# A graph layer on one core: the node loops' stores on SyncE's queue, merged weight loads, and a new layout of the node loops' tiles

## The chip, the cores and the metric

The kernel runs on one NeuronCore of a Trainium2 chip. A core has a tensor engine (TensorE, PE in the profile) for matmuls into PSUM (eight banks of 2 KiB per partition), VectorE (DVE), ScalarE (ACT) and GpSimd (POOL) for elementwise work, and SyncE (SP), which only issues DMAs. Each engine runs its own list of instructions in order, and they wait for each other by semaphores. The metric is the device time of one execution in microseconds; lower is better. All data are float32.

## The reference

The input is x, 32 graphs of 512 nodes with 256 features, and adj, a 0/1 matrix of 512 by 512 for each graph. With h = relu(layernorm(x)), the layer computes:

```python
h1 = relu(bn(conv1d(h, conv1_w)))                     # width 1
x_conv = relu(bn(conv1d(h1, conv2_w, pad=8)) + h)     # width 17
s = h @ w_se.T + b_se                                 # 3 numbers a node
A = exp(-|s_n - s_m|^2) * adj                         # 512 x 512 for each graph
x_nmp = A @ relu(h @ w_msg.T + b_msg)
gi = concat(x_conv, x_nmp) @ w_ih.T + b_ih
gh = h @ w_hh.T + b_hh
r, z = sigmoid(gi_r + gh_r), sigmoid(gi_z + gh_z)
n = tanh(gi_n + r * gh_n)
out = x + (1 - z) * n + z * h
```

## The kernel before

The 32 graphs ("blocks") are worked on in two groups of 16 (NG = 2, GB = 16). The wide convolution is done by frequency: windows of 64 tokens are transformed to 80 rows, two rows make a unit (40 units), each unit is multiplied by its own 256 x 256 complex weight matrix, and the result is transformed back in the last part.

The program runs through five stretches. `first_part(0)` normalises and transforms blocks 0 to 15 and also brings the convolution weights to frequency: it stores them to DRAM (`wd`) from tiles `wst`. `nodes(0)` does the message passing of these blocks and, between it, the products of 36 units. `first_part(1)` does blocks 16 to 31, the four left units of group 0, and combines the gate weights in tiles `w4` and `w7`, from where they go to DRAM (`ws`). `nodes(1)` does the second group with all its 40 units. Then a loop over 16 pairs of blocks computes the gates. The change concerns the two node loops.

The order of the work is written out by hand (`manual_schedule`): each engine's instructions, and the DMAs of each queue, stand in the order in which the Python code names them. What the framework adds is semaphores and the places of tiles. Tiles with one tag of a pool share its buffers, and tags get their places in the order in which they are first asked for. A pool opened after another was closed takes its memory, and the first writer of a new tile waits for what still used the old tile in the same bytes. So the pool `nodes`, where adj, msg, st, sl, sr, A and at live, starts where `w2p` and then `wst` lay in the phase before the first loop, and where `x`, `h1`, `w4` and `w7` lay before the second.

In the node loop (lines 1037 to 1133), `todo` lists the 16 blocks. For each block: `load_adj` brings adj (four DMAs of 256 KB), `load_h` brings the transposed h, `by_chunks` copies it in another order to hq (ScalarE), `message` (L442 to L446) makes msg and the three features st, `features` puts them into fl and fr (VectorE), `factors` transposes these (psl, psr) and copies them to sl and sr (ScalarE), `exponents` makes the exponentials A, `turn` transposes adj to at and `masked` multiplies A by it (VectorE), `block_sums` forms sums of blocks of A and msg (GpSimd, L517), `aggregate7` multiplies them with seven block products instead of eight (L542 to L562) into nmp, and `save_nmp` stores nmp. The last blocks of the second loop use `aggregate` without sums. The work on the next blocks (`more[0]`, `more[1]`, ...) is laid between the matmuls of the present one.

Units are laid between: `multiply(u)` runs `product` (matmuls L390, the result y finished by ScalarE and VectorE), prepares unit u + 2 on GpSimd (wsum L357 and both L370), and loads the weights of a later unit into one of three buffers wt. The store of y is put into a list `stores`, and `flush()` issues what is in it. All stores of y (L400 to L404, issued in L1053) and of nmp (L565) are issued by ScalarE; all loads by SyncE:

```python
store = partial(nc.scalar.dma_start, YD[g][:, 2 * u : 2 * u + 2, :], y)   # L400
nc.scalar.dma_start(ND[b], NMP.pop(b))                                    # L565
nc.sync.dma_start(t[:, k], WD[2 * u + k, : D * D]...)                     # L353, k = 0, 1
```

Buffers: adj 2, msg 3, st 2, wt 3, y 3, hq 2, hT 2, nmp 1.

Of the kernel before, what the change touches and what calls it, by code (L numbers as in the profile page):

```python
# [15 lines left out]
P = 128  # L16
# [49 lines left out]
def gnn_layer(  # L66
# [282 lines left out]

    def load_unit(g, u, pool=wts):  # L350
        t = WT[g, u] = pool.tile([P, 2, DC, D], FP, tag="wt", name=f"wt_{g}_{u}")
        for k in range(2):
            nc.sync.dma_start(t[:, k], WD[2 * u + k, : D * D].rearrange("(p i o) -> p i o", i=DC, o=D))  # L353

    def sum_unit(pw, g, u):
        t = WSUM[g, u] = pw.tile([P, DC, D], FP, tag="wsum", name=f"wsum_{g}_{u}", bufs=2)
# [15 lines left out]
    def product(pw, g, u, xf, later=None):  # L372
        if u > 0 and (g, u) not in BOTH or (g, u) not in WT:
            prepare(pw, g, u, xf)
        wt = WT.pop((g, u))
        re, im = factors_of(xf, u)
        wr, wi = wt[:, 0], wt[:, 1]

        y = pw.tile([P, 2, D], FP, tag="y", name=f"y_{g}_{u}", bufs=3)
        p = bank(f"py_{g}_{u}")  # L380
        k1, k2 = p[:, :D], p[:, D:]
        if u == 0:
            terms = [(k1, re, wr), (k2, im, wi)]
        else:
            both, wsum = BOTH.pop((g, u)), WSUM.pop((g, u))
            k3 = bank(f"py2_{g}_{u}")[:, :D]
            terms = [(k1, re, wr), (k2, im, wi), (k3, both, wsum)]
        for dst, v, w in terms:
            for ic in range(DC):
                nc.tensor.matmul(dst, v[:, ic, :], w[:, ic, :], start=(ic == 0), stop=(ic == DC - 1))  # L390
        y_re, y_im = (by_half(y[:, k, :]) for k in range(2))
        if u == 0:
            nc.scalar.copy(y_re, halves(k1))
            nc.scalar.copy(y_im, halves(k2))
        else:
            nc.scalar.copy(y_re, halves(k1))
            nc.scalar.mul(y_im, halves(k1), -2.0)
            nc.vector.tensor_sub(y_re, y_re, halves(k2))
            nc.vector.tensor_add(y_im, y_im, halves(k3))
        store = partial(nc.scalar.dma_start, YD[g][:, 2 * u : 2 * u + 2, :], y)  # L400
        if later is None:
            store()
        else:
            later.append(store)  # L404

    def load_adj(b):
        ADJ[b] = pools["nodes"].tile([P, N // 32, P], FP, tag="adj", name=f"adj_{b}", bufs=2)

        rows = adj[b].rearrange("(j r) (g m) -> g r j m", r=32, g=4)
        for g in range(4):  # L410
            nc.sync.dma_start(ADJ[b][32 * g : 32 * (g + 1)], rows[g])

    def load_h(b):
        HT[b] = work.tile([P, DC, N], FP, tag="hT", name=f"hT2_{b}")
        nc.sync.dma_start(HT[b], HD[b])
# [13 lines left out]

    def message(b, halves=range(2)):  # L430
        if 0 in halves:
            MSG[b] = pools["nodes"].tile([P, NC, D], FP, tag="msg", name=f"msg_{b}", bufs=3)
            ST[b] = pools["nodes"].tile([P, 2, NC, NS], FP, tag="st", name=f"st_{b}", bufs=2)
        hq = HQ[b]
        h = NC // 2
        for c0 in (h * k for k in halves):
            m = MSG[b][:, c0 : c0 + h, :]
            for j in range(h):
                c = c0 + j
                p = bank(f"pm_{b}_{c}")  # L440
                for ic in range(DC):
                    nc.tensor.matmul(p[:, : D + NS], hq[:, ic, c * P : (c + 1) * P], wmsg[:, ic, :],  # L442
                                     start=(ic == 0), stop=(ic == DC - 1))
                nc.vector.tensor_add(ST[b][:, 0, c, :], p[:, D : D + NS], bmsg[:, D:])
                nc.vector.tensor_add(m[:, j, :], p[:, :D], bmsg[:, :D])
            nc.scalar.activation(m, m, AF.Relu)  # L446
        if 1 in halves:
            del HQ[b]
# [11 lines left out]
    def factors(b):  # L460

        p = bank(f"psl_{b}")
        nc.tensor.transpose(p[:, :P], fl.rearrange("p c k -> p (c k)"), ident)
        t = SL[b] = pools["nodes"].tile([P, P], FP, tag="sl", name=f"sl_{b}", bufs=2)
        nc.scalar.copy(t, p[:, :P])
        p = bank(f"psr_{b}")
        for c in range(NC):
            nc.tensor.transpose(p[:, c * P : (c + 1) * P], fr[:, c].rearrange("p g k -> p (g k)"), ident)  # L468
        t = SR[b] = pools["nodes"].tile([P, N], FP, tag="sr", name=f"sr_{b}", bufs=2)
        nc.scalar.copy(by_chunk(t), chunks(p))  # L470
# [91 lines left out]
        nc.vector.tensor_add(c21, p1, y)  # L562

    def save_nmp(b):
        nc.scalar.dma_start(ND[b], NMP.pop(b))  # L565

# [304 lines left out]
    def store(p, j, queues, t=slice(0, N)):  # L873
        js = slice(t.start // 32, t.stop // 32)
        for g in range(4):
            queues[g % len(queues)].dma_start(quarter(out[2 * p + j], g)[:, js], XP[p][j][32 * g : 32 * (g + 1), js])
# [126 lines left out]
    with tc.tile_pool(name="freq", bufs=1) as fpool:  # L1003
# [33 lines left out]
        def nodes(g, xf, units, last, following=()):  # L1037


            b1 = (g + 1) * GB  # L1040
            pw = pools["pw"]
            todo = [b1 - 1, b1 - 2] + list(range(g * GB, b1 - 2))
            loads = [u for u in (*units, *following) if (g, u) not in WT]
            stores = []

            def load_units(n):
                for _ in range(n):
                    if loads:
                        load_unit(g, loads.pop(0))

            def flush():
                while stores:
                    stores.pop(0)()  # L1053

            def multiply(u):
                product(pw, g, u, xf, stores)
                if u + 2 in units:
                    prepare(pw, g, u + 2, xf)
                load_units(1)

            load_adj(todo[0])
            load_units(3 - sum((g, u) in WT for u in units))
            load_adj(todo[1])
            load_h(todo[3])
            message(todo[0])
            features(todo[0])
            for step in message_sums(todo[0]):
                step()
            message(todo[1], [0])
            factors(todo[0])  # L1070
            message(todo[1], [1])
            features(todo[1])
            exponents(todo[0])
            by_chunks(todo[2])
            turn(todo[0], [0, 1])
            masked(todo[0], [0, 1])
            turn(todo[0], [2, 3])
            masked(todo[0], [2, 3])
            prepare(pw, g, units[1], xf)
            for step in affinity_sums(todo[0]):  # L1080
                step()
            for i, b in enumerate(todo):
                mine = spread(units, i, last) if i < last else []
                more = todo[i + 1 : i + 5]
                seven = i <= last

                def bring():
                    if len(more) > 1:
                        message(more[1])
                        flush()  # L1090
                        features(more[1])

                if g + 1 < NG and i == GB // 2:
                    load_x(b1)
                if g + 1 < NG and i == 3 * GB // 4:
                    statistics(b1)
                if len(more) > 1:
                    load_adj(more[1])
                if len(more) > 3:
                    load_h(more[3])  # L1100
                if more:
                    factors(more[0])
                flush()
                if i == 0:
                    bring()
                for u in mine[:1]:
                    multiply(u)
                if i > 0:
                    bring()
                if not seven:  # L1110
                    aggregate(b, [0])
                if more:
                    turn(more[0], [0, 1])
                    exponents(more[0])
                    masked(more[0], [0, 1])
                for u in mine[1:2]:
                    multiply(u)
                if more:
                    turn(more[0], [2, 3])
                    masked(more[0], [2, 3])  # L1120
                if seven:
                    aggregate7(b)
                else:
                    aggregate(b, [1])
                flush()
                if len(more) > 2:
                    by_chunks(more[2])
                save_nmp(b)
                if more and i + 1 <= last:
                    block_sums(more[0])  # L1130
                for u in mine[2:]:
                    multiply(u)
            flush()
# [105 lines left out]
```

## Time and profile before

The median of three runs is 1842.39 us (1841.37 to 1847.45); the profiled execution has a span of 1842.2 us.

| engine | busy us | share of the span | instructions |
|---|---|---|---|
| PE (matmul) | 1804.6 | 98% | 6974 |
| DVE | 1240.2 | 67% | 2370 |
| POOL | 776.0 | 42% | 731 |
| ACT | 622.0 | 34% | 1252 |

| stretch of the program | from about, us | to about, us |
|---|---|---|
| first_part(0) | 0 | 157 |
| nodes(0) | 157 | 455 |
| first_part(1) | 455 | 572 |
| nodes(1) | 572 | 877 |
| gates, pair by pair | 877 | 1842 |

The DMAs that the change touches, from the table of DMA issues (queue, number, size, median time from issue to landing):

| DMA | queue | count | KB each | us to landing |
|---|---|---|---|---|
| wt from wd | SyncE | 160 | 256 | 4.9 |
| adj | SyncE | 128 | 256 | 6.1 |
| y to yd | ScalarE | 80 | 256 | 3.6 |
| nmp to nd | ScalarE | 32 | 512 | 5.3 |
| hT from hd | SyncE | 28 | 512 | 7.0 |

Busy counts only work of the engines; issuing a DMA, waiting for a semaphore and branches are not in it. A line of the timeline gives the start, the duration, engine and code line, operation, output and inputs with the number of instructions, and in brackets the idle time just before it with what ended it. Instructions that overlap are merged in such a line, so its duration can be a little longer than the distance to the next start. PE records are halves: a float32 matmul of the code counts as two.

### The profile page before, as it was taken

Reading aid. Unit: us, or ns where it says so; the run is one execution under the profiler, and the core shown is the slowest. Engines: PE = TensorE matmul, PEld = TensorE weight load, DVE = VectorE, ACT = ScalarE, POOL = GpSimd, SP = SyncE. Lnnn points to the kernel's source line nnn. Section 1 sums busy time; section 2 is a strip of 40 time slices with the busy share of each in tenths; the row PEclk is TensorE's granted clock in tenths of the full one; section 3 lists DMA queues with packets and bytes.
Section 4 is the critical chain, followed back from the end, with each engine's and each line's share of the span. In section 5 each row is a group of like instructions: output and inputs, shape, how many; then the busy total and the mean of one; then the engine's idle time right before and its main releaser. Section 6 shows DMA issues by size and latency. Waiting matters only on the chain.

```text
span 1842.2 us, 21281 instructions
## 1 busy us (share of the span) xinstructions
PE 1804.6 (98%) x6974; PEld 1157.9 (63%) x6974; DVE 1240.2 (67%) x2370; ACT 622.0 (34%) x1252; POOL 776.0 (42%) x731
## 2 busy tenths in 40 slices
PE   8999999999998899999999999999999999999998
PEld 6777788887897788886545554555455544555444
DVE  7876688886895677886266456655666466645666
ACT  4555444443345444443212221222122221222121
POOL 3432588686433677677321323133222322132221
PEclk9999999999999999999999999999999999999999
DMA  9999787874677778778322443234422442244312
GB/s 258 309 288 219 198 249 203 236 222 146 229 240 190 209 214 240 239 220 298 98 86 39 116 120 101 62 78 120 120 82 39 120 120 91 45 105 120 111 24 54
DMA packets 308370, 288.28 MB, mean 156 GB/s; under 512 B 148044, under 2 KB 238700, under 8 KB 307876
## 3 DMA queue, kind: packets, MB, share of 16 engines
q1 hardware_dynamic: 282676, 224.74, 45.6%
q10 hardware_dynamic: 18992, 38.68, 5.9%
q0 software_dynamic: 6592, 23.50, 4.0%
q8 instruction: 56, 0.92, 0.2%
q14 instruction: 54, 0.44, 0.1%
HBM read 190.45 MB, written 96.40 MB: 156 GB/s over the span
## 4 chain that ended last, share of the span: by engine, by line
PE 89%; DVE 3%; DMA 3%; issue 2%; POOL 2%; ACT 1%; SPq 0%; ACTq 0%; DVEq 0%; POOLq 0%
PE pg L668 30%; PE pn L668 15%; PE py L390 10%; PE pn L542 9%; PE pm L442 5%; PE pc L326 5%; PE pc L656 5%; PE px L341 3%; PE pd L486 2%; PE pw L254 2%; PE phT L310 1%; PE pz L668 1%; PE psr L468 1%; DMA wt<-wd 1%; POOL ts L517 0%
## 5 line engine op out<-in xcount | busy, mean ns | idle before, releaser
L646 POOL TENSOR_TENSOR hp<-hp 128x512 f32<-128x512 f32 x64 | 80.5, 1269 | 413.5 <-DMA hp<-hd 352.3
L668 PE MATMUL pg<-hp,sw 128*128 128x512 f32 x434 | 221.8, 593 | 0.7 <-DVE rz L687 0.5
L668 PE MATMUL pg<-cp,sw 128*128 128x512 f32 x434 | 221.6, 592 | 0.0
L668 PE MATMUL pg<-np,sw 128*128 128x512 f32 x434 | 221.6, 592 | 0.0
L646 POOL TENSOR_TENSOR cp<-cp 128x512 f32<-128x512 f32 x64 | 80.5, 1269 | 231.5 <-ACT cp L662 230.3
L357 POOL TENSOR_TENSOR wsum<-wt 128x512 f32<-128x512 f32 x78 | 102.6, 1315 | 130.9 <-DMA wt<-wd 112.7
L390 PE MATMUL py<-wt,xf 128*128 128x256 f32 x640 | 156.3, 387 | 1.3 <-DMA wt<-wd 1.3
L683 ACT ACTIVATE rz<-rz,brz 128x512 f32<-128x512 f32 x93 | 67.0, 721 | 260.2 <-DVE rz L687 260.2
L668 PEld LDWEIGHTS pg<-hp,sw 128*128 128x128 f32 x434 | 82.2, 190 | 104.8 <-issue 96.9
L668 PEld LDWEIGHTS pg<-cp,sw 128*128 128x128 f32 x434 | 82.5, 190 | 103.8 <-issue 103.8
L668 PEld LDWEIGHTS pg<-np,sw 128*128 128x128 f32 x434 | 82.5, 190 | 103.8 <-issue 103.8
L390 PEld LDWEIGHTS py<-wt,xf 128*128 128x128 f32 x640 | 118.1, 192 | 37.9 <-issue 18.2
L442 PE MATMUL pm<-wmsg,hq 128*128 128x259 f32 x512 | 124.2, 396 | 4.2 <-ACT hq L427 3.9
L807 ACT ACTIVATE nt<-nt,vech 128x512 f32<-128x512 f32 x64 | 46.2, 722 | 236.5 <-DVE nt L806 236.5
L326 PE MATMUL pc<-w,hT 128*128 128x256 f32 x512 | 117.8, 383 | 0.8 <-DVE hT L314 0.8
L668 PE MATMUL pn<-cp,sw 128*128 128x512 f32 x224 | 114.4, 592 | 0.0
L668 PE MATMUL pn<-hp,sw 128*128 128x512 f32 x224 | 114.4, 592 | 0.0
L668 PE MATMUL pn<-np,sw 128*128 128x512 f32 x224 | 114.4, 592 | 0.0
L442 PEld LDWEIGHTS pm<-wmsg,hq 128*128 128x128 f32 x512 | 100.1, 197 | 22.0 <-ACT hq L427 4.8
L492 DVE TENSOR_TENSOR A<-A,at 128x512 f32<-128x512 f32 x128 | 107.7, 880 | 7.6 <-ACT A L488 7.5
L326 PEld LDWEIGHTS pc<-w,hT 128*128 128x128 f32 x512 | 94.6, 190 | 24.0 <-issue 7.2
L656 PEld LDWEIGHTS pc<-back,yt 128*128 128x128 f32 x640 | 92.7, 190 | 7.7 <-issue 7.7
(173 smaller groups left out, 3434.5 us busy)
## 6 DMA issues: line engine op xcount, KB each, us to landing
wt<-wd SPq DMA_DIRECT2D x160, 256.0 KB, 4.9
adj<-in_adj_dram SPq DMA_DIRECT2D x128, 256.0 KB, 6.1
wd<-wst SPq DMA_DIRECT2D x64, 320.0 KB, 5.7
yd<-y ACTq DMA_DIRECT2D x80, 256.0 KB, 3.6
yt<-yd SPq DMA_DIRECT2D x30, 640.0 KB, 6.9
hd<-hT SPq DMA_DIRECT2D x32, 512.0 KB, 4.9
nd<-nmp ACTq DMA_DIRECT2D x32, 512.0 KB, 5.3
xb<-in_x_dram SPq DMA_DIRECT2D x128, 128.0 KB, 3.6
```

Of the source, the lines that this page charges most:

```text
L326: nc.tensor.matmul(p[:, j, :], HT[b][:, ic, c * P : (c + 1) * P], w1[:, ic, :], start=(ic == 0), stop=(ic == DC - 1))
L341: nc.tensor.matmul(p[:, j * 2 * L : (j + 1) * 2 * L], H1[b][:, c0 + j, ic * P : (ic + 1) * P], fwd, start=True, stop=True)
L357: nc.gpsimd.tensor_tensor(t, WT[g, u][:, 0], WT[g, u][:, 1], op=ALU.add)
L390: nc.tensor.matmul(dst, v[:, ic, :], w[:, ic, :], start=(ic == 0), stop=(ic == DC - 1))
L442: nc.tensor.matmul(p[:, : D + NS], hq[:, ic, c * P : (c + 1) * P], wmsg[:, ic, :], start=(ic == 0), stop=(ic == DC - 1))
L492: nc.vector.tensor_mul(A[b][:, mc, :], A[b][:, mc, :], AT.pop((b, mc)))
L542: nc.tensor.matmul(bk, left[:, k, :], right[:, k, :], start=(first and k == 0), stop=(k == 1), skip_group_check=True)
L646: nc.gpsimd.tensor_tensor(t[:, dst, :], t[:, a, :], t[:, b, :], op=sub)
L656: nc.tensor.matmul(bk[:, t0:t1], YT[p][j][:, c, oc * P : (oc + 1) * P], back[:, n : n + t1 - t0], start=(c == 0), stop=(c == len(spans) - ...
L668: nc.tensor.matmul(bk[:, t], sw[:, k, q, o, :], terms[k][q][:, t], start=(first and i == 0), stop=(i == len(ks) - 1), skip_group_check=True)
L683: nc.scalar.activation(rz[:, g, j, :], src, AF.Sigmoid, bias=brz[:, g : g + 1], scale=1.0)
L807: nc.scalar.activation(n, n, AF.Tanh, bias=b_in[:, i : i + 1], scale=1.0)
```

## The change

It has four parts. Within the node loops, the stores of y and nmp are issued by SyncE instead of ScalarE, and the points where the list of stores is emptied are moved so that they stand in step with the loads: at the start of each `multiply` and after the loads at the head of an iteration. The two weight matrices of a unit come in one DMA of 512 KB instead of two of 256 KB. The tiles of the pool `nodes` are laid anew: adj has two tags with one buffer each instead of one tag with two, st is asked for before msg, and the first `message` is named before the second `load_adj`; so the order in memory is adj0, st, msg, adj1, then the rest as before. And at the head of the loop `by_chunks(todo[2])`, which makes hq for the third block, stands before the second half of the second block's message instead of after the first block's exponents. The aim is that loads aren't held up by stores of another queue, that ScalarE isn't held up by a store whose data aren't ready, and that the first tiles of a node loop don't lie where the phase before it was still storing. No arithmetic changes.

```diff
     def load_unit(g, u, pool=wts):
         t = WT[g, u] = pool.tile([P, 2, DC, D], FP, tag="wt", name=f"wt_{g}_{u}")
-        for k in range(2):
-            nc.sync.dma_start(t[:, k], WD[2 * u + k, : D * D].rearrange("(p i o) -> p i o", i=DC, o=D))
+        nc.sync.dma_start(t.rearrange("p k i o -> p k (i o)"),
+                          WD[2 * u : 2 * u + 2, : D * D].rearrange("k (p n) -> p k n", n=DC * D))
...
-        store = partial(nc.scalar.dma_start, YD[g][:, 2 * u : 2 * u + 2, :], y)
         if later is None:
-            store()
+            nc.scalar.dma_start(YD[g][:, 2 * u : 2 * u + 2, :], y)
         else:
-            later.append(store)
-
-    def load_adj(b):
-        ADJ[b] = pools["nodes"].tile([P, N // 32, P], FP, tag="adj", name=f"adj_{b}", bufs=2)
+            later.append(partial(nc.sync.dma_start, YD[g][:, 2 * u : 2 * u + 2, :], y))
+
+    def load_adj(b, slot):
+        ADJ[b] = pools["nodes"].tile([P, N // 32, P], FP, tag=f"adj{slot}", name=f"adj_{b}", bufs=1)
...
     def message(b, halves=range(2)):
         if 0 in halves:
+            ST[b] = pools["nodes"].tile([P, 2, NC, NS], FP, tag="st", name=f"st_{b}", bufs=2)
             MSG[b] = pools["nodes"].tile([P, NC, D], FP, tag="msg", name=f"msg_{b}", bufs=3)
-            ST[b] = pools["nodes"].tile([P, 2, NC, NS], FP, tag="st", name=f"st_{b}", bufs=2)
...
     def save_nmp(b):
-        nc.scalar.dma_start(ND[b], NMP.pop(b))
+        nc.sync.dma_start(ND[b], NMP.pop(b))
...
             def multiply(u):
+                flush()
                 product(pw, g, u, xf, stores)
...
-            load_adj(todo[0])
+            load_adj(todo[0], 0)
             load_units(3 - sum((g, u) in WT for u in units))
-            load_adj(todo[1])
+            message(todo[0])
+            load_adj(todo[1], 1)
             load_h(todo[3])
-            message(todo[0])
             features(todo[0])
...
             factors(todo[0])
+            by_chunks(todo[2])
             message(todo[1], [1])
             features(todo[1])
             exponents(todo[0])
-            by_chunks(todo[2])
...
                     if len(more) > 1:
                         message(more[1])
-                        flush()
                         features(more[1])
...
-                    load_adj(more[1])
+                    load_adj(more[1], i % 2)
                 if len(more) > 3:
                     load_h(more[3])
+                flush()
                 if more:
                     factors(more[0])
-                flush()
...
-                flush()
                 if len(more) > 2:
                     by_chunks(more[2])
-                save_nmp(b)
+                stores.append(partial(save_nmp, b))
```

## The prediction

> **What bounds the kernel now.** I read the engine table first: the tensor engine (PE) is busy 1804.6 us of 1842.2, and no other engine above 67%. What can be won without taking matmuls away is the other 37.6 us, and the slow matmuls that follow an idle stretch. So I next read the table of stretches, to see where those 37.6 us lie.
>
> ```profile
> core 0: us, PE busy (x) PEld busy (x) DVE busy (x) ACT busy (x) POOL busy (x), PEclk, DMA share, GB/s
> 150.00:190.00 40.00, 37.44 (x185) 29.67 (x184) 24.61 (x65) 21.41 (x48) 12.42 (x12) 0.91 0.93 201
> ...
> 190.00:250.00 60.00, 56.10 (x259) 45.41 (x258) 45.85 (x90) 23.98 (x55) 44.06 (x42) 0.94 0.75 214
> ...
> 250.00:300.00 50.00, 50.00 (x241) 40.98 (x240) 42.92 (x91) 24.97 (x59) 38.87 (x38) 1.00 0.88 241
> ...
> 400.00:455.00 55.00, 51.96 (x236) 42.86 (x236) 39.69 (x73) 20.03 (x53) 39.98 (x38) 0.94 0.50 159
> ...
> 573.00:600.00 27.00, 21.90 (x95) 16.19 (x94) 16.33 (x53) 12.23 (x27) 9.41 (x10) 0.87 1.01 215
> 600.00:650.00 50.00, 44.98 (x214) 36.60 (x213) 32.48 (x72) 21.01 (x49) 30.65 (x30) 1.00 0.72 210
> ```
>
> In the steady part of a node loop (250 to 300 us) PE is never idle: nothing can be won there. The loss lies at the two entries, at 150 to 210 and 573 to 625 us, and at one place near the end of the first loop. The next view is the timeline around each, one engine at a time; the bracket at a line's end is the idle time before it and what ended it.
>
> ```profile
> 160.68 0.16 DVE L444 TENSOR_TENSOR st<-pm,bmsg 128x3 f32<-128x3 f32 x1 [7.00 <-DMA wd<-wst]
> 169.57 6.69 PE L442 MATMUL pm<-wmsg,hq 128*128 128x259 f32 x16 [1.92 <-ACT hq L427]
> 195.04 1.31 POOL L357 TENSOR_TENSOR wsum<-wt 128x512 f32<-128x512 f32 x1 [15.08 <-DMA wt<-wd]
> 204.40 2.08 PE L542 MATMUL pn<-ts,ms 128*128 128x256 f32 x4 [1.20 <-POOL ts L517]
> 427.74 0.27 ACT L465 COPY sl<-psl 128x128 f32<-128x128 f32 x1 [6.69 <-DVE nmp L562]
> 428.55 2.09 PE L486 MATMUL pd<-sr,sl 9*128 9x512 f32 x8 [3.04 <-ACT sr L470]
> 578.03 0.16 DVE L444 TENSOR_TENSOR st<-pm,bmsg 128x3 f32<-128x3 f32 x1 [9.57 <-DMA ws<-w]
> 623.70 1.13 PE L390 MATMUL py<-wsum,both 128*128 128x256 f32 x4 [2.71 <-POOL both L370]
> ```
>
> Last, the waits of SyncE's own queue, for what holds the loads back: line, what it waited for, us in all, times, longest.
>
> ```profile
> SPq L411 <- DMA nd<-nmp: 50.7, 14, 6.8
> ...
> SPq L353 <- DMA yd<-y: 39.6, 6, 12.5
> ...
> SPq L353 <- DMA nd<-nmp: 29.3, 6, 7.6
> ```
>
> Loads wait for the landing of stores from which they read nothing. In the program as built, hardware DMAs of both queues take eight semaphores in turn, and a DMA waits until the one eight places earlier in program order has landed. SyncE issues ahead, ScalarE reaches its stores late, so the load eight places on stands still until then.
>
> **What the skill says.** "TensorE: Matmul & The Clock Gate", section "What's actually happening": after an idle window the array runs at half clock until about 3.4 us of work have passed. The trace shows the half clock but already after 1.9 us of idle (6.69 us for a group that later takes 3.67). "Perfetto Trace Analysis", section "Tensor Engine Instruction": ScalarE and VectorE are strict queues. The trace agrees: at 427 us ScalarE's copy of sl stood 6.69 us behind the nd store. "SBUF — State Buffer", section "SBUF: two separate sides": GpSimd and VectorE exclude each other on a shared port. It agrees too: near 424 us an add of L557 took 1.49 us, against 0.42 at 604 us. "DMA: Bandwidth & Descriptors", section "Issuing engines are not separate DMA queues": issuing from two engines saves only issue time. By that, moving stores costs no bandwidth; the trace of before cannot show it.
>
> **The losses, one by one.** Idle time plus slow matmuls, from start-to-start times against the same groups later.
> A, entry 1: 0.64 (psl) and 1.92 idle; the pm group of 16 takes 6.52 instead of 3.5. Sum 5.6.
> B, 198 to 210: 2.70 and 1.20 idle, then three pn groups in 5.3 instead of 2.6. Sum 6.6.
> C, 425: 3.04 idle, then 6.85 for three groups instead of 3.67. Sum 6.2.
> D, entry 2: 3.15 and 1.95 idle; pm of 8 takes 3.32 instead of 1.76, pm of 16 5.20 instead of 3.5, and pd 0.2 more. Sum 8.5.
> E, 609 to 624: 1.09, 0.23, 0.98 and 2.71 idle. Sum 5.0.
> Together 31.9 us.
>
> **The change, part by part.**
> *Layout.* From the start of the pool, adj takes 0 to 16 KiB of a partition, msg 16 to 28, st follows at 28. In the phase ahead of the first loop, wst buffers hold 16 to 48 KiB, and the one at 28 to 32 is stored last: st waits until 160.6 us. Ahead of the second, a w7 buffer lies at 22 to 32.5: st waits for its ws store, to 577.9. Anew, adj0 takes 0 to 8, st 8 to 8.2, msg 8.2 to 20.2, adj1 20.2 to 28.2, and sl starts at 28.2 as before. At 8 KiB lay w2p (last read at 151.7) and, in the second phase, h1 of block 30 (its px matmuls are the first half of the 32 from 567.6 to 572.0). So st is free, and VectorE follows the pm matmuls: fl is ready at about 161.7 and 576.5, before PE asks (162.6 and 577.4). The wait moves to adj1, whose loads must await the same stores (160.6, which its place in the queue, 164.8, hides; 577.9 instead of 575.9, 2 us), and sl still waits until 577.9: 0.5 us after its psl, hidden by message(todo[1], [1]), 1.76 us of matmuls.
> *by_chunks(todo[2]) earlier.* The two copies of hq (1.16 us) ran after the four exponents, and PE waited for them. Now they stand right after sr, in a time when ScalarE waits for VectorE anyway (1.17 us at 164.2). Cost nothing; with the layout it removes A and D, 14.1 us.
> *Stores on SyncE.* (76 + 32) issues of 0.33 us leave ScalarE: 35 us, but ScalarE is busy 34% and its order is what counted: C goes, 6.2 us, for sl no longer stands behind nd. On SyncE they add 108 issues; 80 product-weight issues go with the merged loads, so the queue is hardly longer. The new wait: a store waits for VectorE, and behind it stand the next wt and adj loads. The y store is queued ahead of the next product, whose wt load waits for that product's matmuls, later than y. The nd store is at worst 5 us behind PE (nmp was finished at 427.3, its matmuls at 422.2), and a wt load behind it is wanted three products on: two of 2.6 us and one aggregate of 6 us at least. Hidden. nmp has one buffer: its store must land (median 5.3 us) before the next aggregate's second copy, 11 us on; hidden but at the crowded entries.
> *Loads no longer wait for ScalarE's stores.* At entry 1 the wt load of the fourth unit went at 188.8, after y had been stored at 186.3; GpSimd waited for it till 195.0, and its block sums made PE wait (B). At entry 2 it went at 606.1 (E). In step, it goes when its buffer's product is done and the loads ahead are issued, about 175 and 590, and lands about 184 and 598 (8 to 10 us there, as adj took 7.4 to 9.8). After landing GpSimd needs 12.3 us to the fourth unit's both (611.4 to 623.7); PE wants it 12 us after the first aggregate, which ends at about 182 and 596.5 without A and D. So B goes, E to about 2 us.
> *One DMA for a product's weights.* Same bytes, half the issues. The trace has no 512 KB load of wt; a 512 KB hT load took 7.0 us in the median against 4.9 for a half of wt, and two halves issued 0.5 us apart end at 5.4. The load is 0 to 1.6 us later; three buffers hide it. I take nothing.
> **Sum.** 31.9 less what I keep back for the crowded entries: 2 (nd and adj in step, B), 2 to 3 (E), so 5 in all. 1842.4 - 26.9 = 1815.5; I say 1815.
>
> **Rivals.**
> 1. *The entries are bound by the DMA engines.* Share 0.93 and 1.01 in the stretches above; adj14 issued at 164.8 landed only about 9.8 us later. Then VectorE, freed of st, waits for adj instead, PSUM banks stay full, and PE waits there. Against it: PE has some 10 us of matmuls that need no adj. C goes, and half of the other 25.7: 1842 - 6 - 13 = 1823.
> 2. *Waits take each other's place.* Only C and a third of the rest go, for GpSimd's chain of 12 us is the real limit at B and E: 1842 - 6 - 8 = 1828.
> 3. *The stores block the loads.* One in-order queue, 29 iterations with products; if nd's late 5 us reach PE by 1.5 us in each, it is + 43 on - 27: 1858, slower. For it: SPq already waits long. Against it: PE is at 100% in steady state with loads that waited for the same stores.
> 4. *Nothing*: the gaps belong to the data's way and come back whole: 1842.
>
> **How the numbers follow.** Forecast (1808 to 1820) 0.58; rival 1 0.17, rival 2 0.12, rival 3 0.07, rival 4 0.03, and 0.03 for more than all I count. Below 1807 would need more than the 31.9 and some of the tail's 2.7 at 867 us; above 1832 are rivals 3 and 4 and little of 2. Range 1807 to 1832. Faster 0.90, same 0.03, slower 0.07.
>
> **What would show it.** L444's idle before its first instruction under 1 us at both entries; no "DMA yd" or "DMA nd" among the long waits of SyncE's loads; sl behind no nmp; stretches 150 to 190 and 573 to 600 at over 97% PE. Wrong if PE's waits name wt or adj in the steady part, if ScalarE waits for nd's landing before L549, or if the first aggregate of a loop starts at its old time (181.7, 599.5).

## The result, and the profile after

| | median us | range | runs |
|---|---|---|---|
| before | 1841.88 | 1840.27 to 1847.45 | 4 |
| after | 1827.09 | 1826.38 to 1828.32 | 4 |

The ratio is 0.9915 (95%: 0.9893 to 0.9937): the change is worth 15 us of the 27 that were forecast. The time lies within the range of 1807 to 1832, 12 us above the point and outside the 1808 to 1820 that had the highest chance. A profile is one execution: that of before took 1843.99 us, that of after 1826.61, so the traces differ by 17.4 us of span (1842.2 to 1824.8), 2.6 more than the medians.

The engine table of the page after says that nothing was saved but idle and slow time of PE: 1804.6 us busy has become 1796.3, with the same 6974 matmuls.

```profile
PE 1796.3 (98%) x6974; PEld 1152.3 (63%) x6974; DVE 1244.0 (68%) x2370; ACT 623.0 (34%) x1252; POOL 779.1 (43%) x731
```

The table of stretches, in the same columns as before (PE, PEld, DVE, ACT and POOL busy with counts, PEclk, DMA share, GB/s). The stretches are fixed in time, and the work has moved up by some microseconds. Two rows of before stand first, which the prediction doesn't show.

```profile
300.00:350.00 50.00, 50.00 (x239) 40.89 (x238) 39.33 (x88) 23.99 (x57) 36.67 (x36) 1.00 0.84 233
...
700.00:750.00 50.00, 50.00 (x245) 42.17 (x244) 41.72 (x82) 22.54 (x56) 35.28 (x35) 1.00 0.75 229
```

After:

```profile
150.00:190.00 40.00, 40.00 (x210) 31.44 (x209) 28.18 (x78) 23.20 (x53) 15.39 (x15) 1.00 1.07 240
190.00:250.00 60.00, 56.65 (x272) 45.87 (x271) 49.59 (x100) 27.56 (x65) 49.88 (x48) 1.00 0.89 230
...
300.00:350.00 50.00, 48.30 (x237) 40.11 (x239) 40.80 (x86) 21.98 (x52) 37.49 (x35) 1.00 0.91 226
...
400.00:455.00 55.00, 54.55 (x252) 45.03 (x250) 38.65 (x83) 18.45 (x46) 40.75 (x40) 0.97 0.55 186
...
573.00:600.00 27.00, 25.34 (x113) 19.50 (x111) 20.67 (x50) 10.54 (x25) 16.29 (x16) 0.94 1.11 236
600.00:650.00 50.00, 49.42 (x240) 41.44 (x237) 42.31 (x80) 23.67 (x57) 36.57 (x37) 1.00 0.78 228
...
700.00:750.00 50.00, 47.99 (x234) 40.15 (x233) 34.24 (x77) 21.76 (x54) 36.75 (x36) 1.00 0.88 243
```

Several things are to be seen. At entry 1 (150 to 190) PE is at 100%, where over 97% was forecast, but at entry 2 (573 to 600) at 94%. At 190 to 250 it is idle nearly as long as before, 3.35 us against 3.90. And two stretches in which PE was never idle before, 300 to 350 and 700 to 750, have lost 1.7 and 2.0 us. The timeline of PE shows the places (start, duration, operation, in brackets the idle time before and what ended it); the code lines from 401 on are one lower than before.

```profile
175.75 1.89 PE L541 MATMUL pn<-A,msg 128*128 128x256 f32 x8
...
199.43 1.13 PE L541 MATMUL pn<-ts,ms 128*128 128x256 f32 x4 [1.26 <-ACT nmp L550]
...
340.28 1.13 PE L541 MATMUL pn<-ts,ms 128*128 128x256 f32 x4 [1.70 <-ACT nmp L550]
...
417.14 1.13 PE L485 MATMUL pd<-sr,sl 9*128 9x512 f32 x4 [0.45 <-DVE nmp L559]
418.20 2.71 PE L390 MATMUL py<-wt,xf 128*128 128x256 f32 x8
420.70 1.91 PE L390 MATMUL py<-wsum,both 128*128 128x256 f32 x4
...
578.16 1.09 PE L485 MATMUL pd<-sr,sl 9*128 9x512 f32 x2 [1.66 <-DVE msg L444]
579.18 3.26 PE L390 MATMUL py<-wt,xf 128*128 128x256 f32 x8
...
583.56 1.89 PE L541 MATMUL pn<-A,msg 128*128 128x256 f32 x8
...
720.51 1.13 PE L390 MATMUL py<-wsum,both 128*128 128x256 f32 x4 [2.01 <-POOL both L370]
```

The first aggregates start at 175.75 and 583.56; before it was

```profile
181.68 1.89 PE L542 MATMUL pn<-A,msg 128*128 128x256 f32 x8
...
599.48 1.89 PE L542 MATMUL pn<-A,msg 128*128 128x256 f32 x8
```

To compare kernels whose work is shifted, I read a **period** from this view: the time from the start of one aggregate to the next. Undisturbed, it is 16.55 us in loop 1 (two products between) or 19.14 (three; all of loop 2), and 13.04 at C, where the next block's message is already made (this last one is seen in the trace of the experiment e4 alone). What exceeds these is lost. With the entries measured from the first message matmul (157.22 and 572.02 before, 156.33 and 560.51 after) to the first aggregate, the whole difference of the two traces can be laid out:

| place | forecast gain | before us | after us | gain us |
|---|---|---|---|---|
| A, entry 1 | 5.6 | 24.46 | 19.42 | 5.0 |
| B, period at 198 | 6.6, less 2 | 23.68 | 20.32 | 3.4 |
| C, period at 425 | 6.2 | 19.24 | 16.13 | 3.1 |
| other periods of loop 1 | 0 | | | 0.4 |
| D, entry 2 | 8.5 | 27.46 | 23.05 | 4.4 |
| E, first period of loop 2 | 2 to 3 (2 in the sum) | 25.19 | 19.14 | 6.1 |
| three later periods of loop 2 | 0 | 19.13 to 19.14 | 19.98, 19.96, 21.42 | -3.9 |
| end of loop 2 | 0 | | | -0.6 |
| outside the loops | 0 | | | -0.5 |
| sum | 26.9 | | | 17.4 |

About five us are missing at the five places, and 4.6 were given back elsewhere. Who ended PE's waits stands in the table of waits (us in all, times, longest):

```profile
PE py L390 <- POOL both L370: 3.2, 3, 2.0
PE pn L541 <- ACT nmp L550: 3.0, 2, 1.7
...
PE pd L485 <- DVE msg L444: 1.7, 1, 1.7
```

**The wait of 1.70 us at 340** is followed back over three engines. VectorE finished nmp at 325.09:

```profile
324.67 0.42 DVE L561 TENSOR_TENSOR nmp<-p,pn 128x256 f32<-128x256 f32 x1
```

SyncE's queue (start and time taken by the issue) had already begun the next loads by then; the nd store stands behind them and leaves at 331.06, 6 us after its data were ready:

```profile
320.91 6.43 SPq L410 DMA_DIRECT2D adj<-in_adj_dram  x4
327.43 3.06 SPq L414 DMA_DIRECT2D hT<-hd  x1
330.53 0.43 SPq L1052 DMA_DIRECT2D yd<-y  x1
331.06 0.38 SPq L564 DMA_DIRECT2D nd<-nmp  x1
```

nmp has one buffer, so ScalarE's second copy out of PSUM stands until the store has landed, and PE waits for the banks:

```profile
339.58 0.37 ACT L548 COPY nmp<-pn 128x256 f32<-128x256 f32 x1 [3.18 <-DMA nd<-nmp]
```

The same happens at 198 (nmp done at 184.7, stored at 190.55, ScalarE waiting 4.99 us until 198.73); there GpSimd had also waited 8.06 us for weights until 187.39, and its block sums cost PE 0.49 and 1.23 us before. That is what remains of B.

**The wait of 2.01 us at 720** is GpSimd's chain again, now in the middle of a loop. A weight load left at 699.56, behind adj (2.72 us of issue) and hT (2.80), and GpSimd could start only at 708.16. (The bracket names PE's py; the landing of wt, at 708.00, is what came last.)

```profile
708.16 1.27 POOL L357 TENSOR_TENSOR wsum<-wt 128x512 f32<-128x512 f32 x1 [6.38 <-PE py L390]
...
719.23 1.22 POOL L370 TENSOR_TENSOR both<-xf 128x256 f32<-128x256 f32 x1
```

From 708.16 to the end of `both` are 12.3 us, the same chain that was measured before the change at 611.4 to 623.7. The adj and hT loads had themselves been late: until 692.2 the queue had stood 6.9 us at the nd store of the block before, whose data VectorE had not finished. Such waits are new, and are among the longest of SyncE now. Most of them fall into slack, this one did not.

```profile
SPq L564 <- DVE nmp L561: 117.7, 22, 7.0
...
SPq L1052 <- DVE y L399: 64.9, 25, 9.6
```

**What remains of D** is a wait for adj that the wait for st had hidden. VectorE follows the message matmuls now (its first st waits for PE, not for the ws store) and then stands still for the first adj:

```profile
561.77 0.16 DVE L443 TENSOR_TENSOR st<-pm,bmsg 128x3 f32<-128x3 f32 x1 [4.82 <-PE pm L441]
...
572.75 1.30 DVE L474 STREAM_TRANSPOSE at<-adj 128x512 f32<-128x512 f32 x2 [3.32 <-DMA adj<-in_adj_dram]
```

### The profile page after: what moved, and what is told of

The parts are those of the page before. It is cut to its first block, busy times and chain, and to the rows that moved or that the text cites. A ratio compares the mean times of both kernels' runs of the same rounds, so it can differ in the third digit from the quotient of the medians.

```text
span 1824.8 us, 21188 instructions
## 1 busy us (share of the span) xinstructions
PE 1796.3 (98%) x6974; PEld 1152.3 (63%) x6974; DVE 1244.0 (68%) x2370; ACT 623.0 (34%) x1252; POOL 779.1 (43%) x731
## 4 chain that ended last, share of the span: by engine, by line
PE 84%; DMA 5%; DVE 4%; POOL 2%; issue 2%; SPq 1%; ACT 1%; ACTq 0%; DVEq 0%; POOLq 0%
PE pg L667 30%; PE pn L667 15%; PE py L390 8%; PE pn L541 8%; PE pc L326 5%; PE pc L655 5%; PE pm L441 4%; PE px L341 3%; DMA wt<-wd 2%; PE pw L254 2%; PE phT L310 1%; PE pd L485 1%; DMA nd<-nmp 1%; PE pz L667 1%; DVE A L491 1%
## 5 line engine op out<-in xcount | busy, mean ns | idle before, releaser
L441 PE MATMUL pm<-wmsg,hq 128*128 128x259 f32 x512 | 118.5, 383 | 1.0 <-DVE nmp L559 1.0
L491 DVE TENSOR_TENSOR A<-A,at 128x512 f32<-128x512 f32 x128 | 113.6, 925 | 6.0 <-ACT A L487 6.0
L441 PEld LDWEIGHTS pm<-wmsg,hq 128*128 128x128 f32 x512 | 96.2, 190 | 17.2 <-DVE nmp L559 2.5
```

Of the source, the lines that this page charges most:

```text
L491: nc.vector.tensor_mul(A[b][:, mc, :], A[b][:, mc, :], AT.pop((b, mc)))
```

## The experiments

My theory after the traces: the gain comes from the stores standing in step with the loads, and what is missing was lost to the order within the one queue, in which nd, y and wt stand behind adj and hT. The rivals: the layout made the gain; the move off ScalarE made it; the merged weight load took it back. Each ratio is to runs of the kernel before on the same chip. A single trace can lie some us off its kernel's median (that of e2 lies 9 us below, of e4 7 below, of e7 and e9 5 above), so sizes are taken from the ratios and places from the traces.

| kernel | median us (range) | ratio (95%) |
|---|---|---|
| e1: before with layout and by_chunks | 1838.71 (1830.36 to 1846.80) | 0.9984 (0.9973 to 0.9995) |
| e7: after without layout and by_chunks | 1828.73 (1827.55 to 1833.87) | 0.9918 (0.9904 to 0.9932) |
| e6: after with two weight loads | 1827.01 (1821.42 to 1829.12) | 0.9904 (0.9887 to 0.9920) |
| e2: after, its stores on ScalarE | 1830.53 (1821.26 to 1834.85) | 0.9934 (0.9911 to 0.9956) |
| e3: after, nd at its old place | 1823.08 (1819.08 to 1825.54) | 0.9893 (0.9876 to 0.9910) |
| e4: after, stores before loads | 1821.02 (1814.33 to 1825.33) | 0.9875 (0.9856 to 0.9894) |
| e5: after, stores and weights before loads | 1818.29 (1816.05 to 1819.75) | 0.9868 (0.9851 to 0.9885) |
| e8: e5 with an earlier ws store | 1813.71 (1811.23 to 1814.25) | 0.9835 (0.9820 to 0.9849) |
| e9: e8 without layout and by_chunks | 1818.53 (1816.33 to 1823.08) | 0.9856 (0.9839 to 0.9873) |

### e1 and e7: is it the layout?

e1 is the kernel before with the layout's parts of the diff alone; e7 is the kernel after with them undone. The core of the edit, as e1 has it:

```diff
-        ADJ[b] = pools["nodes"].tile([P, N // 32, P], FP, tag="adj", name=f"adj_{b}", bufs=2)
+        ADJ[b] = pools["nodes"].tile([P, N // 32, P], FP, tag=f"adj{slot}", name=f"adj_{b}", bufs=1)
...
             factors(todo[0])
+            by_chunks(todo[2])
             message(todo[1], [1])
             features(todo[1])
             exponents(todo[0])
-            by_chunks(todo[2])
```

> The kernel before with the new layout and the earlier by_chunks(todo[2]) alone; all stores stay on ScalarE, weights in two DMAs. Theory 1 (each wait had its own cause): losses A and D go, as in the changed kernel: first aggregate of loop 1 at about 176 instead of 181.7, of loop 2 about 11 us nearer to its entry less what adj's landing costs there (4.4 gained in the changed kernel); B, C and E stay, for the loads still wait for yd and nd: about 1842 - 5 - 4.5 = 1832. Theory 2 (waits take each other's place): what is won at the first aggregate is lost again at B and E, because GpSimd's weights still come after the first y stores: 1838 to 1842.

> The changed kernel with the old layout and the old place of by_chunks(todo[2]); stores in step on SyncE and merged loads stay. Theory 1 (causes add up): A and D come back, 5 and 4.4 us: 1835 to 1838. Theory 2 (the layout alone won 3 us, because what it won at the first aggregate was lost behind; the stores in step won the rest by themselves): 1829 to 1832.

Alone, the layout brings 3 us (1 to 5). On top of the stores in step it brings 0.6 us, give or take 5. Yet in the traces both entries respond as forecast: e1's first aggregate comes after 19.37 us and e7's after 23.27, and in e7 VectorE waits again, 6.97 us for the wd store and 10.75 us for the ws store. PE's timeline of e1 shows where the gain of entry 1 went:

```profile
191.75 1.97 PE L390 MATMUL py<-wt,xf 128*128 128x256 f32 x8 [1.77 <-DMA wt<-wd]
194.45 1.13 PE L390 MATMUL py<-wsum,both 128*128 128x256 f32 x4 [0.73 <-POOL both L370]
...
199.01 1.13 PE L542 MATMUL pn<-A,msg 128*128 128x256 f32 x4 [2.56 <-POOL A L517]
201.36 2.07 PE L542 MATMUL pn<-ts,ms 128*128 128x256 f32 x4 [1.22 <-POOL ts L517]
```

Counted from the first message matmul, the weights come only 2 us earlier than before (GpSimd starts on them at 192.46, before at 195.04), so PE, which arrives 5 us earlier, waits for them longer. The sum from the first message matmul to the third aggregate says it in one number: 64.68 us before, 62.63 in e1, 56.29 after, 56.36 in e7. In these traces the old layout, in step, costs nothing by the third aggregate, for in e7 B is gone (its period is 16.54): the 5 us are lost once, at A or at B. At entry 2 the layout is worth more (to the second aggregate 52.65, 44.82, 42.19 and 47.66 us in the same order).

### e6: one weight load or two

```diff
-        nc.sync.dma_start(t.rearrange("p k i o -> p k (i o)"),
-                          WD[2 * u : 2 * u + 2, : D * D].rearrange("k (p n) -> p k n", n=DC * D))
+        for k in range(2):
+            nc.sync.dma_start(t[:, k], WD[2 * u + k, : D * D].rearrange("(p i o) -> p i o", i=DC, o=D))
```

> The changed kernel with a unit's weights in two DMAs of 256 KB again. Theory 1 (the merge costs and wins nothing that shows): 1825 to 1829. Theory 2 (each DMA takes one of eight places in the order of completions, and 2.3 more in an iteration make the loads at its head wait longer): SyncE waits longer for earlier DMAs, 1830 to 1836.

The ratios overlap nearly whole (two loads are 2 us better, give or take 5): merging the loads is worth nothing that can be measured, as the prediction took it.

### e2 and e3: is it the queue?

e2 keeps the new places of the stores in the order of the program, but gives them back to ScalarE; e3 gives back nd alone, to its old place.

```diff
-            later.append(partial(nc.sync.dma_start, YD[g][:, 2 * u : 2 * u + 2, :], y))
+            later.append(partial(nc.scalar.dma_start, YD[g][:, 2 * u : 2 * u + 2, :], y))
...
-        nc.sync.dma_start(ND[b], NMP.pop(b))
+        nc.scalar.dma_start(ND[b], NMP.pop(b))
```

> The changed kernel with the stores of y and nmp given back to ScalarE at the places in the order where the change has put them; only the queue differs. Theory 1 (the queue counts): the loads wait again for the landing of stores that ScalarE reaches late, and sl stands behind the nd store at the head of every iteration, so VectorE's late nmp hits PE: 1835 to 1850, and long waits of SyncE for yd and nd come back. Theory 2 (the places count, not the queue): within 3 us of the changed kernel, 1824 to 1830.

> The changed kernel with the nd store back on ScalarE, right after by_chunks as before; y stays on SyncE. Theory 1 (the nd store, last in line behind the loads at the head of an iteration, is what gives back part of the gain: it leaves 6 us after nmp is done, and the next nmp waits for its landing): PE's 3.0 us of waits for nmp go with their slow matmuls, and wt loads no longer stand behind nmp, so POOL both shrinks; but C may return (up to 6 us) when VectorE is late: 1820 to 1828. Theory 2 (GpSimd and VectorE are late by themselves): no change but for C: 1827 to 1834.

e2 keeps most of the gain, 0.9934 against 0.9915, a difference that its interval doesn't tell from none. "DMA: Bandwidth & Descriptors" of the Trainium skill, section "Issuing engines are not separate DMA queues", agrees in so far as the queue alone moves little. But the waits for landings that the first theory named are back in its trace, and yet most of the gain stays:

```profile
SPq L414 <- DMA nd<-nmp: 49.3, 10, 8.5
...
SPq L352 <- DMA nd<-nmp: 8.1, 1, 8.1
```

What differs from before is who waits: mostly the hT and adj loads. The wt loads stood 68.9 us for yd and nd before the change and stand 11.4 us here. That suggests that not the sum of these waits counts, but which loads they hold. C is where the queue counts: in e2's table of waits it has come back,

```profile
PE pd L485 <- ACT sr L469: 3.0, 1, 3.0
```

and e3 has sl behind a late nmp too, while no kernel with nd on SyncE has. But e3 isn't slower than after (0.9893 against 0.9915, 4 us, give or take 5). In its trace C takes 17.83 us against 16.13, and PE waits for no nmp copy, for which it waited 3.0 us in after: nd on SyncE, at the place that the change gave it, lost elsewhere about what it won at C. With e1, e6 and e2 the gain is left to the new places of the stores; this is by elimination, for no run has these places alone.

### e4, e5 and e8: the order within the queue

e4 puts `flush()` ahead of the loads at the head of an iteration. e5 goes further: the stores, then the first product with its weight load, then adj and hT. e8 is e5 with the ws store named ahead of the hT load at the end of first_part(1).

```diff
-                if len(more) > 1:
-                    load_adj(more[1], i % 2)
-                if len(more) > 3:
-                    load_h(more[3])
                 flush()
...
                 for u in mine[:1]:
                     multiply(u)
+                if len(more) > 1:
+                    load_adj(more[1], i % 2)
+                if len(more) > 3:
+                    load_h(more[3])
                 if i > 0:
                     bring()
```

e8, on top:

```diff
             if b == b1 - 1:
                 by_chunks(b - 1)
-                load_h(b0)
             for step in one:
                 step()
+            if b == b1 - 1:
+                load_h(b0)
```

> The changed kernel with only the stores put ahead of adj and hT at the head of an iteration; the first weight load stays behind them. It splits the gain of the run with weights first (1818.3, against 1827.1). Theory 1a (the late nd store is the fault): ScalarE no longer waits for nd's landing at L548, PE's 3.0 us for nmp and the slow matmuls after them go: 1820 to 1823. Theory 1b (the late weight load is the fault): GpSimd still waits some 90 us for weights in all, and PE for both: 1825 to 1828.

> The changed kernel with the head of an iteration put in another order: first the stores, then the first product's weight load, then adj and hT. Theory 1 (stores and weight loads are late because five loads that nobody wants soon stand ahead of them): PE's waits for nmp (3.0 us) and for both (3.2 us) go, with the slow matmuls behind them: 1818 to 1822. Theory 2 (VectorE and GpSimd set the rest): 1826 to 1829. If adj then comes too late, VectorE waits for adj at the turns: over 1830.

> The kernel with weights first (1818.3), and in first_part(1) the last ws store of 1.3 MB named ahead of load_h of the group's first block, which holds the queue until ScalarE has made hq. ws is then stored some 5 us earlier and no longer shares the DMA engines with the first adj of the second loop, for which VectorE waited 3.2 us. Theory 1 (adj's landing at entry 2 is what is left of D): the wait for adj and the 1.6 us of PE before pd go, with the slow matmuls: 1814 to 1817. Theory 2 (the entry is bound by all its DMA bytes, not by their order): 1817 to 1819.

e4 wins 7 us on after (give or take 5), e5 9 (5), e8 another 6 (4). Between e4 and e5 lies 1 us, give or take 5: that the stores' place is worth time is shown, of the weights' place only the waits below. In the traces no wait of ScalarE for nd's landing at L548 is left in any of the three. In e5 SyncE waits for nmp ahead of the loads (166.6 us in all, so there is slack for it), and the store leaves when it is ready:

```profile
323.50 0.32 SPq L564 DMA_DIRECT2D nd<-nmp  x1
324.83 0.41 SPq L352 DMA_DIRECT2D wt<-wd  x1
325.29 2.90 SPq L410 DMA_DIRECT2D adj<-in_adj_dram  x4
328.29 3.25 SPq L414 DMA_DIRECT2D hT<-hd  x1
```

The first adj load leaves 4.4 us later than in after, and VectorE waits for none of these four. What the weights' place does is seen in GpSimd's wait for them (us in all, times, longest). After:

```profile
POOL wsum L357 <- DMA wt<-wd: 90.4, 27, 9.0
```

e5:

```profile
POOL wsum L357 <- DMA wt<-wd: 22.0, 8, 5.0
```

It was 112.7 us before and is 78.8 in e4, where PE still waits 1.3 us for `both`; in e5 PE waits for it nowhere. But before the change was made GpSimd waited longest of all, and PE was at 100% in the steady part: 16.55 or 19.14 us of matmuls cover the chain of 12 us and part of the wait, and only the rest is paid.

e5 keeps the 1.56 us of PE at entry 2. In after the ws store goes out at 559.05 behind an hT load, and the eight adj loads from 560.90, 0.4 us after the first message matmul; in e8 ws is issued at 547.39 and adj from 554.21, 1.2 us ahead of that matmul. Whether the earlier ws or the earlier adj loads did it, e8 doesn't separate. VectorE's wait for adj, PE's wait and the slow products are gone; e8's timeline of PE against that of after above:

```profile
568.48 1.89 PE L390 MATMUL py<-wt,xf 128*128 128x256 f32 x8
570.30 1.14 PE L485 MATMUL pd<-sr,sl 9*128 9x512 f32 x8
571.37 2.00 PE L390 MATMUL py<-wt,xf 128*128 128x256 f32 x8
573.20 1.03 PE L390 MATMUL py<-wsum,both 128*128 128x256 f32 x4
574.07 1.89 PE L541 MATMUL pn<-A,msg 128*128 128x256 f32 x8
```

Entry 2 takes 18.62 us, against 23.05 after and 27.46 before. e8 beats both kernels. That it lies at 1813.7 us, near the 1815 of the forecast, is chance: the forecast was for the order of after.

### e9: the layout once more, in a good order

e9 is e8 with e7's edit.

> Version with weights and stores ahead of the loads (1813.7 us), but with the old layout of the tiles (adj in one tag of two buffers, st after msg), the old place of the first message and of by_chunks(todo[2]): what are layout and by_chunks worth once the queue is in a good order? Theory W (what they win at a loop's entry was eaten in the version after by the late weights and the late nd store behind them, and so is kept when those are early): PE loses the 5 us of each entry again, time 1819 to 1825 us, ratio 0.988 to 0.991, VectorE waits about 7 and 10 us again before the first st of the two loops. Theory N (an early first aggregate only waits longer for what comes next, whatever the order): 1812 to 1816 us, the same as with the new layout, ratio 0.983 to 0.985, and the stretch behind the first aggregate is shorter by what the entry is longer.

The result lies between the two: e8 is 4 us faster, with an interval of 4 either way, which leans to the layout's gain being kept but doesn't settle it. The traces lean the same way: to the third aggregate of loop 1 53.43 us in e8 and 56.63 in e9, to the second of loop 2 37.76 and 41.62. One part of the expectation was wrong: VectorE waits 7.20 us at entry 1 again, but not for the ws store at entry 2, since ws goes out early enough in this order for the old place of st as well.

## Why the prediction was right, and where it was off

The direction was right, and in the main for the reason given, the stores in step with the loads. That the time fell within the range owes much to the width of the range, which was drawn to hold two of the rivals; the sum itself was 12 us too low.

- **Direction and rank.** Right. The losses lay where the table of stretches showed them, the long waits of loads for yd and nd are gone from SyncE's table, sl stands behind no nmp, and nothing moved in the gates' part (965.4 us in both). Of the other signs, two were met in part: VectorE's first st of a loop still comes after 4.63 and 4.82 us of idle, but PE's matmul ends it and no store, and 573 to 600 reached 94% and not 97%. And one sign of being wrong came: ScalarE waited for nd's landing at L548, 8.2 us in two waits.
- **Layout and by_chunks, "it removes A and D, 14.1 us".** The term is 9.4 in the trace (5.0 and 4.4), and as a gain of the whole only 3 alone and 0.6, give or take 5, on top of the rest. A was sized rightly at its place, but A and B are one slack, which the traces of e1 and e7 show. D was mis-sized by 4.1: the waits for st and for adj ran side by side, and I priced adj1's later loads at nothing while the wait for the first adj, which rival 1 named, came next.
- **C, 6.2.** ScalarE's block is gone, as forecast. 3.1 remain: 0.45 us of PE idle for a bank that VectorE empties, and then slow matmuls. That a second cause stood close behind was not in the prediction. In e4's trace the period is 13.04 and nothing remains. In e5 and e8 PE is idle for 0.46 and 0.45 us at the same place, and the same slow matmuls follow (16.30 and 16.29); why VectorE is late there and not in e4 is open.
- **B, 4.6 after what was kept back.** 3.4. The weight load was forecast to go at about 175 and land at 184; it went at 177.45, behind adj and hT, and landed at 187.26, 9.8 us later; GpSimd had it at 187.39. Then nd's landing came on top.
- **E, 2 to 3.** 6.1, whole: under-sized.
- **"The nd store is at worst 5 us behind PE ... Hidden."** This step failed. I asked what stands behind nd, and not what nd stands behind: five loads whose issue took 9.6 us. With one buffer of nmp it cost PE 3.0 us, half of the 6.2 us that PE is still idle in loop 1; e4 removed it. Likewise wt behind adj and hT, which cost 3.9 us in loop 2 and went in e5 (1.8 are left in e4's trace). In e2's trace, where wt stands behind adj and hT as well but behind no store that waits for VectorE, loop 2 loses nothing there, so the waiting store has its part in it. "Two products and one aggregate" of slack held for most loads, not for all.
- **Merged loads at nothing.** Right (e6).
- **Rivals.** Rival 2, waits taking each other's place, is the nearest, in time (1828) and for A and B. Its time is met by luck: it took C whole and a third of the rest, and C went by half and E whole. Rival 1 is right for entry 2 alone, and there the order of the loads (e8) did away with the wait. Rival 3 is right in kind, small in size: stores and loads do hold each other up in the one queue, at three or four places and not in 29 iterations. That I gave 0.58 to a sum of losses taken as independent was the weak point.

## What to carry to other kernels

Losses that lie behind one another on the same path are not a sum: ask of each wait that is removed which other wait was running beside it or starts a few us later, and count the slack once. When a store moves into the queue of the loads, ask in both directions: what stands behind it, and what it stands behind, and how many buffers hang on its landing. In such a queue, order by the time until the data are needed: the stores that free a single buffer and the loads with the longest chain behind them go ahead of loads that are wanted an iteration later.

## What had not been expected of the hardware

How long PE was idle in one piece does not decide whether the next matmuls are slow. After 0.45 us at 417 the eight matmuls that usually take 1.73 from start to start took 2.50; after 1.26, 1.70 and 2.01 us at 199, 340 and 720 they ran at their usual pace at once. The granted clock (PEclk, the number behind the busy times) shows a pattern. In the node loops of all eleven traces it is halved for 3.41 us or for 6.83, and within one trace the starts lie whole multiples of 3.41 us apart (419.33 and 579.76 in after, 47 times 3.41). So the time can be cut into stretches of 3.41 us on this grid:

```profile
415.92:419.33 3.41, 2.96 (x13) 1.33 (x10) 3.41 (x8) 2.12 (x4) 3.41 (x5) 1.00 0.32 121
419.33:422.75 3.42, 3.42 (x9) 2.69 (x9) 2.74 (x4) 0.71 (x3) 3.42 (x3) 0.50 0.93 272
```

In the first of these PE was idle for only 0.45 us, but 1.89 us of it were pd, whose matmuls use 9 of 128 rows each. The 2.01 us at 720 lie on both sides of a boundary, 1.21 and 0.80. Counted over all eleven traces from 60 us on, every stretch at full clock with more than 2.24 us of idle time and pd together was followed by half clock, and none with less than 1.92. It is an observation, which no experiment tested. "TensorE: Matmul & The Clock Gate" of the Trainium skill, section "What's actually happening", says that the clock goes by a free-running window of 3413 ns; the traces agree. They differ from an idle window in that 0.45 us of idle time was enough, and in e5, before a half clock at 174.65, 0.04 us with 2.23 us of pd. The slow matmuls at 169.57, which the prediction put after 1.92 us of idle time, fit as well: the half clock began at 168.70, after 1.05 us of it.

And loads can hold the queue far longer than usual: four adj loads take 2.1 to 2.7 us of SyncE between 630 and 710 us, and 6.43 at 320.91. The queue waited there, from 320.0 on, 2.9 us in three pieces for adj loads that hadn't landed, and two of the four issues took 1.66 and 1.91 us. A store in the same queue pays for it.
